# A softmax with fewer vector operations and a new set of starting places in a planned decoder layer

## The chip, the cores and the metric

The kernel runs on one core of one Trainium2 chip. The metric is the device time of one execution in microseconds, as the median of three runs. All arithmetic is in float32.

## The reference

One decoder layer on x of shape (16, 256, 256), with a context of the same shape. Three parts follow each other, each added to its input and then normalised over the last axis.

```python
x = layernorm(x + attn(x))            # a causal, weighted running mean
x = layernorm(x + xattn(x, ctx, ctx)) # correlation by FFT, the 5 best shifts
x = layernorm(x + ffn(x))             # 8 experts, two branches, a router
```

The change touches two softmax-like places. In the first part, the scores are a column slice of the input projection after a causal convolution of four taps with a bias, times a scale for each of the 32 heads, limited and exponentiated:

```python
z = conv(x @ in_proj_w, conv_w) + conv_b       # 4 taps for each channel
s_raw = z[..., -K:]                            # one score for each of 32 heads
p = exp(clip(score_scale * s_raw, -20.0, 20.0))
# p times a weight over time, and running sums of p*re, p*im and p
```

In the second part, each head has the mean correlation of query and key at every shift; the five largest are kept and their softmax weighs five rolled copies of the values:

```python
w, idx = top_k(corr_mean, 5)
w = softmax(w, axis=-1)
out = sum of w[k] * roll(V, idx[k])
```

## The kernel before

The 16 batch rows are taken as 8 pairs. Each pair goes through seven stages, and each is a function of the pair number:

- `front`: the input projection, the convolutions and the scores. The scores of both rows of a pair lie in one tile `sc` (128 partitions, 256 times). `convolve` does the first tap with its bias on ScalarE and three more taps as three VectorE operations; then come the two scale-and-limit operations, the exponential, the weight over time (`tw`, in the profile `dist`) and the running sum `den`.
- `body`: the running sums of the cosine and sine parts. It holds the heaviest VectorE work: scans, products and one fused step on tiles of 128x1024 (`sn`, `cs`, `ge`). It feeds the matmuls `y` and `ss`, and ends in `out_ps` and a layernorm.
- `context` (place "ctx"): the spectra of the context, matmuls `dft_ps` and `kv_ps`; their results go to HBM for pairs 1 to 7.
- `back`: the loads that bring these spectra back.
- `attention` (place "att"): the spectrum of x, the correlation, `choose` (top five and softmax on tiles of 32 partitions: `corr`, `top`, `m8`, in the profile `m`), and the rolled values.
- `router`: the running sum of x, `h_ps`, and the weights of the experts.
- `experts` (place "expert"): the matmuls `c_ps`, `v_ps` and `u_ps`, the last layernorm, the store.

Weights of the experts are first multiplied together by `fold_weights` (place "fold", matmuls `w_ps`). Setup code ahead of the stages loads the small parameters: `pv` is one tile of 45 columns with convolution taps (`C_CW`), biases (`C_CB`), the scores' scale (`C_SCALE`) and others. Columns 24 to 27 of the taps and column 6 of the biases belong to the scores.

No operation is issued where it is written. The objects `V`, `S`, `G`, `T` and `Y` (VectorE, ScalarE, GpSimd, TensorE, and the SyncE queue of DMAs) note each operation, with a rank. The rank comes from the table `PLACES`: for each stage a length and eight beginnings, one for each pair; the rank of an operation is the beginning plus a share of the length. When everything is noted, `Work.run` plans three times. `forward` walks through time with a cost for each operation and lets each engine take the ready operation with the lowest rank; `backward` goes from the end and works out when each operation is due. The due times are the ranks of the next pass. The plan with the shortest planned span is issued, and each engine then runs its instructions in that order and no other. Table loads of ScalarE are put in where the order needs them.

```python
length, *begin = PLACES[stage]
return begin[pair] + part * length
...
for n in range(passes):
    order, starts, span = self.forward(rank, late)
    if best is None or span < best[0]:
        best = span, order, starts
    rank = late = self.backward(starts, span)
```

Because each operation is issued by `give`, nearly all instructions have the same source line in the profile, L452 (`call(*args, **kw)`); table loads have L450. They are told apart by the names of their tiles. Buffers are few where it matters: two of each of `sn`, `cs` and `ge`, one `y` and one `ss` bank, four banks `fps` shared by the other matmuls.

Of the kernel before, what the change touches and what calls it, by code (L numbers as in the profile page):

```python
# [15 lines left out]
AF = mybir.ActivationFunctionType  # L16
ALU = mybir.AluOpType
# [19 lines left out]


PLACES = {
    "front": (0.95, 1.25, 4.3, 4.1, 4.0, 6.3, 4.8, 6.35, 8.75),  # L40
    "body": (0.35, -1.65, 1.6, 3.25, 1.95, 5.25, 3.85, 7.05, 8.6),
    "ctx": (0.85, 2.48, 1.4, 1.55, 1.9, 4.7, 0.3, 2.05, 2.55),
    "back": (3.4, -8.35, -6.05, -8.95, -7.9, -4.75, -7.45, -5.0, 0.8),
    "att": (0.1, -2.35, -3.95, -2.7, -6.8, 1.0, -0.0, 0.7, 3.5),
    "router": (0.35, 0.35, -2.05, 3.45, 4.3, 6.0, 5.65, 6.85, 5.55),
    "expert": (1.18, 3.85, 3.95, 5.85, 5.8, 8.6, 5.95, 9.15, 13.2),
    "fold": (6.5, 1.66),
}
EARLY, SLABS, XT_BUFS, ZC_BUFS, KBUFS, VBUFS, X_BUFS = 3, 19, 1, 4, 2, 3, 9
AHEAD = range(1, NP)  # L50
# [6 lines left out]
C_CW = 0  # L57
C_CB = 28
C_SLOPE = 35
C_SCALE = 36  # L60
# [53 lines left out]
class Work:  # L114
# [67 lines left out]
    @staticmethod  # L182
    def place(stage, pair, part):
        length, *begin = PLACES[stage]
        return begin[pair] + part * length
# [270 lines left out]
def decoder_kernel(ctx: ExitStack, tc: tile.TileContext, a: dict, out: bass.AP):  # L456
# [5 lines left out]
    V, S, G, T, Y = (  # L462
        Later(work, name, eng)
        for name, eng in (
            ("DVE", nc.vector), ("ACT", nc.scalar), ("POOL", nc.gpsimd), ("PE", nc.tensor), ("SP", nc.sync)
        )
    )
# [16 lines left out]
    def load(name, shape, chunks=False, pool=const, eng=Y, tag=None):  # L484
        t = pool.tile(shape, F32, name=name, tag=tag or name)
        eng.dma_start(out=t, in_=chunked(name) if chunks else a[name])
        return t

    def new(pool, shape, tag, bufs=1, name=None):
        work.apart()  # L490
        return pool.tile(shape, F32, name=name or tag, tag=tag, bufs=bufs)

    def slab(shape, name):
        return new(ff, shape, "slab", SLABS, name)

    def m_bank(name):
        return new(m_ps, [P, 512], "mps", 2, name)

    def f_bank(name):
        return new(f_ps, [P, 512], "fps", 4, name)  # L500

    def split(ps, n=2):
        return ps.rearrange("p (c d) -> p c d", c=n)
# [12 lines left out]
    pv = load("pv", [P, NPV], eng=G)  # L516
# [19 lines left out]
    def cumsums(dst, src):  # L536

        V.tensor_tensor_scan(dst, again[:, : dst.shape[1]], src, 0.0, ALU.mult, ALU.add)
# [17 lines left out]
    S.activation(tw, tw, AF.Exp, scale=sp[:, 0:1])  # L556


    dl = pv[:, C_DL : C_DL + 3]
    dw = const.tile([P, 8], F32, name="dw", tag="dw")  # L560
    V.tensor_reduce(dw[:, 4:5], dl, AX.X, ALU.max)
# [28 lines left out]
    def convolve(zc, ps, ci):  # L590

        cw = pv[:, C_CW + 4 * ci : C_CW + 4 * ci + 4]
        S.activation(zc, ps, AF.Identity, bias=pv[:, C_CB + ci : C_CB + ci + 1], scale=cw[:, 3:4])
        for s in (1, 2, 3):
            V.scalar_tensor_tensor(
                zc[..., s:], ps[..., : L - s], cw[:, 3 - s : 4 - s], zc[..., s:], ALU.mult, ALU.add
            )
# [4 lines left out]
    def front(p):  # L602
        place = lambda f: work.place("front", p, f)
        work.rank = place(0.0)
        xT = [slab([P, 2, L], "xc") for c in range(2)]
        for c in range(2):
            Y.dma_start(out=xT[c], in_=a["xT"][p][:, c])
        work.rank = place(0.2)


        ps = m_bank("sc_ps")
        for c in range(2):
            for par in range(2):
                for j in range(2):
                    q = 32 * (2 * j + par)
                    T.matmul(
                        ps[q : q + 32, :L], w_sc[:, c, par, :], xT[c][:, j, :], start=c == 0, stop=c == 1
                    )
        sc = new(mx, [P, L], "sc")
        convolve(sc, ps[:, :L], 6)  # L620
        V.tensor_scalar(sc, sc, pv[:, C_SCALE : C_SCALE + 1], 20.0, ALU.mult, ALU.min)
        V.tensor_scalar(sc, sc, -20.0, None, ALU.max)
        pw = sc
        S.activation(pw, sc, AF.Exp)
        V.tensor_tensor(pw, pw, tw, ALU.mult)
        den = new(mx, [P, L], "den", 2)
        cumsums(den, pw)
        V.tensor_scalar(den, den, 1e-4, None, ALU.max)

        zcs, gs = [], []  # L630
        for m in range(4):
            work.rank = place(0.4 + 0.15 * m)
            zc = new(mx, [P, 2, L], "zc", ZC_BUFS)
            ps = m_bank("in_ps")
            for c in range(2):
                T.matmul(ps, w_in[:, c, m * P : (m + 1) * P], xT[c], start=c == 0, stop=c == 1)
            convolve(zc, split(ps), m)
            zcs.append(zc)
            if m < 2:
                g = new(mx, [P, 2, L], "g", 3)  # L640
                S.activation(g, zc, AF.Identity, bias=dw[:, 1:2], scale=dw[:, 3:4])
                G.tensor_tensor(g, g, zc, ALU.mult)

                ph = new(mx, [P, 2, L], "ph", PH_BUFS)
                for j in range(2):
                    for u in range(2):
                        Y.dma_start(
                            out=ph[64 * u : 64 * u + 64, j, :],
                            in_=pw.rearrange("(n r) t -> n r t", r=8)[8 * j : 8 * j + 8, 2 * m + u]
                            .unsqueeze(1)  # L650
                            .to_broadcast([8, 8, L]),
                        )
                V.scalar_tensor_tensor(g, g, dw[:, 0:1], ph, ALU.add, ALU.mult)
                gs.append(g)

        for m in (2, 3):
            zc = zcs[m]
            S.activation(zc, zc, AF.Silu)
            gate = zcs[m] = new(mx, [P, 2, L], "gate", 3)
            for j in range(2):  # L660
                for h in range(2):
                    Y.dma_start(out=gate[64 * j : 64 * j + 64, h, :], in_=zc[64 * h : 64 * h + 64, j, :])
        made[p] = zcs, gs, den
# [299 lines left out]
    def choose(prod):  # L963


        NHP = 2 * NH
        ps = f_bank("corr_ps")
        for i in range(3):
            T.matmul(ps[:NHP, :L], prod[:, i, :], c_corr[:, i, :], start=i == 0, stop=i == 2)
        T.matmul(ps[:NHP, L : L + 1], prod[:, 0, :], c_mean, start=True, stop=True)  # L970
        corr = new(at, [NHP, L], "corr")
        top = new(at, [NHP, 8], "top")
        m8 = new(at, [NHP, 8], "m8")
        rest = new(at, [NHP, L], "rest")
        S.copy(corr, ps[:NHP, :L])
        S.copy(top[:, 0:1], ps[:NHP, L : L + 1])
        V.max(m8, corr)
        V.tensor_copy(m5[:, :TOPK], m8[:, :TOPK])
        V.match_replace(rest, m5, corr, -FAR)
        V.tensor_scalar(m8, m8, top[:, 0:1], None, ALU.add)  # L980
        V.tensor_scalar(top[:, 1:2], m8[:, 0:1], -1.0, None, ALU.mult)
        V.tensor_tensor(top[:, 2:3], top[:, 1:2], top[:, 0:1], ALU.add)
        S.activation(m8, m8, AF.Exp, bias=top[:, 1:2])
        S.activation(corr, corr, AF.Exp, bias=top[:, 2:3])
        V.tensor_reduce(top[:, 3:4], m8[:, :TOPK], AX.X, ALU.add)
        V.reciprocal(top[:, 4:5], top[:, 3:4])
        V.scalar_tensor_tensor(corr, rest, -FAR, corr, ALU.is_equal, ALU.mult)

        we = new(at, [NHP, 2, P], "we")
        r = top[:, 4:5]  # L990
        S.activation(corr[:, P:], corr[:, P:], AF.Identity, scale=r)
        V.scalar_tensor_tensor(we[:, 0, :], corr[:, :P], r, corr[:, P:], ALU.mult, ALU.add)
        V.scalar_tensor_tensor(we[:, 1, :], corr[:, :P], r, corr[:, P:], ALU.mult, ALU.subtract)
        ps = f_bank("w_t_ps")
        for c in range(2):
            T.transpose(ps[:, c * NHP : (c + 1) * NHP], we[:, c, :], ident[:NHP, :NHP])
        wT = new(at, [P, 2, NHP], "wT")
        S.copy(wT, split(ps[:, : 2 * NHP]))
        ps = f_bank("w_f_ps")
        for i in range(3):  # L1000
            for o in range(2):
                T.matmul(
                    ps[64 * o : 64 * o + 64, i * NHP : (i + 1) * NHP], f_roll[:, o, i, :], wT[:, o, :],
                    start=True, stop=True,
                )
        wf = new(at, [P, 3, NHP], "wf")
        S.copy(wf, split(ps[:, : 3 * NHP], 3))
        return wf, split(ps[:, : 3 * NHP], 3)
# [201 lines left out]
    for p in range(NP):  # L1210
        for stage in (front, body, context, back, attention, router, experts):
            stage(p)
# [138 lines left out]
```

## Time and profile before

| what | value |
|---|---|
| time, median of 3 runs | 856.03 us (855.74 to 857.06) |
| the profiled execution, its own time | 857.1 us |
| its span, first to last instruction | 855.3 us |
| mean granted TensorE clock | 0.989 |
| TensorE busy | 812.4 us, 95% |
| VectorE busy | 700.0 us, 82% |
| ScalarE busy | 581.8 us, 68% |
| GpSimd busy | 256.9 us, 30% |

A row of the profile gives an engine, an operation, the tile it writes and the tiles it reads, the count, the busy time, the mean of one in nanoseconds, and the engine's idle time just ahead of it with what ended that. PE is TensorE, PEld its weight loads, DVE is VectorE, ACT ScalarE, POOL GpSimd, and SP the SyncE queue. PEclk is the granted TensorE clock, where 1 is full speed. Matmuls overlap each other, so a busy PE can hold small gaps that are not seen as idle.

### The profile page before, as it was taken

Reading aid. Unit: us, or ns where it says so; the run is one execution under the profiler, and the core shown is the slowest. Engines: PE = TensorE matmul, PEld = TensorE weight load, DVE = VectorE, ACT = ScalarE, POOL = GpSimd, SP = SyncE. Lnnn points to the kernel's source line nnn. Section 1 sums busy time; section 2 is a strip of 40 time slices with the busy share of each in tenths; the row PEclk is TensorE's granted clock in tenths of the full one; section 3 lists DMA queues with packets and bytes.
Section 4 is the critical chain, followed back from the end, with each engine's and each line's share of the span. In section 5 each row is a group of like instructions: output and inputs, shape, how many; then the busy total and the mean of one; then the engine's idle time right before and its main releaser. Section 6 shows DMA issues by size and latency. Waiting matters only on the chain.

```text
span 855.3 us, 12062 instructions
## 1 busy us (share of the span) xinstructions
PE 812.4 (95%) x4180; PEld 459.1 (54%) x4180; DVE 700.0 (82%) x1200; ACT 581.8 (68%) x862; POOL 256.9 (30%) x301
## 2 busy tenths in 40 slices
PE   4899989989999999999999999999999999999994
PEld 1355554455345564566445745565457457548453
DVE  5799599989998989998999999998979784472431
ACT  3899749777996798675987698678967632712601
POOL 7541356546122051243301501634004111221000
PEclk9899999999999999999999999999999999999997
DMA  8974675574376346633654456426463601130040
GB/s 270 328 177 107 192 196 170 145 200 124 75 173 144 74 102 145 161 85 59 168 124 110 92 116 150 124 50 163 107 138 66 150 22 47 53 72 1 25 99 25
DMA packets 58572, 103.30 MB, mean 121 GB/s; under 512 B 7744, under 2 KB 24160, under 8 KB 58512
## 3 DMA queue, kind: packets, MB, share of 16 engines
q1 hardware_dynamic: 48912, 71.85, 36.3%
q0 software_dynamic: 9600, 30.69, 11.3%
q8 instruction: 33, 0.54, 0.3%
q14 instruction: 27, 0.22, 0.1%
HBM read 28.06 MB, written 11.53 MB: 46 GB/s over the span
## 4 chain that ended last, share of the span: by engine, by line
PE 65%; DVE 13%; ACT 8%; DMA 7%; issue 4%; POOL 1%; SPq 1%; POOLq 0%; DVEq 0%; ACTq 0%
PE u_ps L452 13%; PE v_ps L452 10%; PE c_ps L452 9%; PE h_ps L452 6%; PE kv_ps L452 4%; DVE cs L452 3%; PE in_ps L452 3%; PE ss L452 3%; PE y L452 3%; ACT cs L452 2%; DVE sn L452 2%; PE q_ps L452 2%; PE out_ps L452 2%; DMA sn<-zc 2%; PE dft_ps L452 2%
## 5 line engine op out<-in xcount | busy, mean ns | idle before, releaser
L452 PE MATMUL c_ps<-fcT,w_c 128*128 128x512 f32 x256 | 120.2, 602 | 1.7 <-DVE dx L452 0.8
L452 PE MATMUL v_ps<-fxT,w_v 128*128 128x512 f32 x256 | 119.3, 600 | 1.7 <-ACT e L452 1.4
L452 PE MATMUL u_ps<-u_o,e 128*128 128x256 f32 x512 | 116.6, 382 | 0.3 <-DVE pp L452 0.3
L450 ACT ACT_TABLE_LOAD x89 | 114.2, 1283 | 1.6
L452 PEld LDWEIGHTS u_ps<-u_o,e 128*128 128x128 f32 x512 | 95.6, 190 | 19.9 <-issue 7.4
L452 DVE TENSOR_TENSOR_SCAN cs<-again,cs 128x1024 f32<-128x1024 bf16 x32 | 77.8, 2432 | 0.0
L452 PEld LDWEIGHTS c_ps<-fcT,w_c 128*128 128x128 f32 x256 | 46.5, 190 | 55.6 <-issue 46.6
L452 DVE SCALAR_TENSOR_TENSOR zc<-in_ps,pv,zc 128x510 f32<-128x510 f32 (+2 forms) x96 | 70.1, 736 | 6.3 <-ACT zc L452 5.6
L452 PEld LDWEIGHTS v_ps<-fxT,w_v 128*128 128x128 f32 x256 | 46.7, 190 | 53.0 <-issue 43.9
L452 DVE TENSOR_TENSOR_SCAN sn<-again,sn 128x1024 f32<-128x1024 bf16 x32 | 74.2, 2320 | 0.2
L452 PE MATMUL in_ps<-xc,in_proj_w 128*128 128x512 f32 x128 | 65.0, 636 | 5.1 <-DVE zc L452 4.9
L452 PE MATMUL kv_ps<-Wkv,specc 128*128 128x512 f32 x128 | 60.6, 608 | 0.9 <-DVE ks L452 0.4
L452 POOL TENSOR_TENSOR pp<-qf,kf 128x512 f32<-128x512 f32 (+1 forms) x32 | 45.1, 1429 | 52.4 <-ACT qf L452 37.3
L452 PE MATMUL h_ps<-fxT,w_h 128*128 128x512 f32 x128 | 59.4, 604 | 0.0
L452 DVE TENSOR_TENSOR e<-e,v_ps 128x512 f32<-128x512 f32 x64 | 43.0, 674 | 17.5 <-PE v_ps L452 17.3
L452 POOL TENSOR_TENSOR t<-vf,wf 128x256 f32<-128x256 f32 x32 | 22.6, 726 | 107.9 <-ACT wf L452 80.9
L452 POOL DMA_DIRECT2D out<-x x16 | 11.7, 731 | 131.9 <-ACT x L452 131.7
L452 POOL TENSOR_TENSOR g<-g,zc 128x512 f32<-128x512 f32 x16 | 24.0, 1497 | 83.0 <-ACT g L452 82.0
L452 ACT ACTIVATE sn<-sn,theta_col 128x512 f32<-128x512 f32 x64 | 44.7, 718 | 5.3 <-DMA sn<-zc 5.3
L452 DVE SCALAR_TENSOR_TENSOR cs<-cs,sn 128x1024 f32<-128x1024 f32 x32 | 40.3, 1259 | 9.2 <-ACT cs L452 9.2
L452 DVE TENSOR_TENSOR sn<-sn,ge 128x1024 f32<-128x1024 f32 x32 | 42.9, 1342 | 5.6 <-DMA ge<-g 3.8
L452 DVE TENSOR_TENSOR cs<-cs,ge 128x1024 f32<-128x1024 f32 x32 | 45.3, 1417 | 0.0
(220 smaller groups left out, 1589.4 us busy)
## 6 DMA issues: line engine op xcount, KB each, us to landing
sn<-zc SPq DMA_DIRECT2D x64, 256.0 KB
ge<-g SPq DMA_DIRECT2D x64, 256.0 KB
wb<-fwT SPq DMA_DIRECT2D x64, 256.0 KB
xc<-in_xT SPq DMA_DIRECT2D x16, 256.0 KB
ct<-in_ctx SPq DMA_DIRECT2D x16, 256.0 KB
x<-in_x POOLq DMA_DIRECT2D x16, 256.0 KB, 4.2
ph<-sc SPq DMA_DIRECT2D x64, 64.0 KB
gate<-zc SPq DMA_DIRECT2D x64, 64.0 KB
```

Of the source, the lines that this page charges most:

```text
L450: self.scalar.preload_act_table_set(self.TABLES[table])
L452: call(*args, **kw)
```

## The change

The scale of the scores is multiplied once, in the setup, into their taps and their bias in `pv`. In `front`, the operation that multiplied by the scale and applied the upper limit goes away, and both limits become one operation. In `choose`, the eight largest values are no longer shifted by the mean correlation; the negated, shifted maximum is worked out in one operation from the unshifted maximum, and the exponential of the eight takes its bias from column 2 instead of column 1 of `top`. All numbers of `PLACES` are replaced as well, save a few that happen to agree, so each of the three planning passes starts from other ranks.

```diff
 PLACES = {
-    "front": (0.95, 1.25, 4.3, 4.1, 4.0, 6.3, 4.8, 6.35, 8.75),
-    "body": (0.35, -1.65, 1.6, 3.25, 1.95, 5.25, 3.85, 7.05, 8.6),
-    "ctx": (0.85, 2.48, 1.4, 1.55, 1.9, 4.7, 0.3, 2.05, 2.55),
-    "back": (3.4, -8.35, -6.05, -8.95, -7.9, -4.75, -7.45, -5.0, 0.8),
-    "att": (0.1, -2.35, -3.95, -2.7, -6.8, 1.0, -0.0, 0.7, 3.5),
-    "router": (0.35, 0.35, -2.05, 3.45, 4.3, 6.0, 5.65, 6.85, 5.55),
-    "expert": (1.18, 3.85, 3.95, 5.85, 5.8, 8.6, 5.95, 9.15, 13.2),
-    "fold": (6.5, 1.66),
+    "front": (1.0, 2.05, 4.35, 3.85, 4.2, 5.55, 6.45, 6.3, 7.95),
+    "body": (0.5, -0.5, 1.55, 3.3, 1.5, 4.5, 4.65, 7.05, 7.6),
+    "ctx": (1.0, 2.03, 0.6, 1.2, 1.55, 3.2, 2.35, 1.7, 2.05),
+    "back": (1.35, -6.65, -5.65, -8.75, -9.0, -4.35, -5.75, -2.55, -0.65),
+    "att": (1.75, -3.0, -3.85, -3.8, -5.45, -2.0, -1.05, -0.75, 1.35),
+    "router": (0, 2.0, -2.7, 3.75, 2.9, 3.85, 6.6, 7.65, 4.35),
+    "expert": (1.23, 3.65, 3.65, 5.65, 6.25, 7.5, 7.5, 10.2, 12.05),
+    "fold": (2.0, 2.26),
 }
...
     S.activation(tw, tw, AF.Exp, scale=sp[:, 0:1])
 
 
+    for lo, n in ((C_CW + 24, 4), (C_CB + 6, 1)):
+        V.tensor_scalar(pv[:, lo : lo + n], pv[:, lo : lo + n], pv[:, C_SCALE : C_SCALE + 1], None, ALU.mult)
...
         convolve(sc, ps[:, :L], 6)
-        V.tensor_scalar(sc, sc, pv[:, C_SCALE : C_SCALE + 1], 20.0, ALU.mult, ALU.min)
-        V.tensor_scalar(sc, sc, -20.0, None, ALU.max)
+        V.tensor_scalar(sc, sc, 20.0, -20.0, ALU.min, ALU.max)
         pw = sc
         S.activation(pw, sc, AF.Exp)
...
         V.match_replace(rest, m5, corr, -FAR)
-        V.tensor_scalar(m8, m8, top[:, 0:1], None, ALU.add)
-        V.tensor_scalar(top[:, 1:2], m8[:, 0:1], -1.0, None, ALU.mult)
+
+        V.tensor_scalar(top[:, 1:2], m8[:, 0:1], top[:, 0:1], -1.0, ALU.add, ALU.mult)
         V.tensor_tensor(top[:, 2:3], top[:, 1:2], top[:, 0:1], ALU.add)
-        S.activation(m8, m8, AF.Exp, bias=top[:, 1:2])
+        S.activation(m8, m8, AF.Exp, bias=top[:, 2:3])
         S.activation(corr, corr, AF.Exp, bias=top[:, 2:3])
```

## The prediction

> **What bounds the kernel now.** I read the page's busy shares and its chain first, then a table of busy time for five stretches, then the waits of TensorE inside two of them, and last the groups of the edited operations.
>
> The page's first part and its chain:
>
> ```profile
> PE 812.4 (95%) x4180; PEld 459.1 (54%) x4180; DVE 700.0 (82%) x1200; ACT 581.8 (68%) x862; POOL 256.9 (30%) x301
> ...
> PE 65%; DVE 13%; ACT 8%; DMA 7%; issue 4%; POOL 1%; SPq 1%; POOLq 0%; DVEq 0%; ACTq 0%
> ```
>
> TensorE bounds the kernel. It is idle for only 855.3 - 812.4 = 42.9 us, and the chain spends 65% on it and 13% on VectorE. The busy time of each engine by stretch says where the 42.9 us lie:
>
> ```profile
> 0.00:42.80 42.80, 27.37 (x95) 11.43 (x96) 28.01 (x65) 24.22 (x34) 28.36 (x49) 0.92 0.94 299
> 42.80:256.60 213.80, 202.45 (x1120) 109.06 (x1119) 194.95 (x272) 177.53 (x281) 90.34 (x105) 0.99 0.60 156
> 256.60:640.00 383.40, 378.80 (x2032) 216.43 (x2031) 357.00 (x617) 295.59 (x413) 105.39 (x105) 1.00 0.50 118
> 640.00:833.80 193.80, 193.57 (x892) 114.25 (x891) 116.80 (x238) 82.06 (x131) 31.32 (x40) 1.00 0.25 59
> 833.80:855.30 21.50, 10.25 (x49) 7.92 (x47) 3.29 (x12) 2.37 (x5) 1.45 (x2) 0.80 0.07 24
> ```
>
> The columns are the stretch, its length, then the busy time of PE, PEld, DVE, ACT and POOL, the granted clock, the DMA share and GB/s. TensorE's idle time is 15.4 us in the start-up, 11.35 in the second stretch (5.3% of it), 4.6 in the third (1.2%), 0.2 in the fourth, and 11.2 in the tail. VectorE is 91% and 93% busy in the second and third stretches and 60% in the fourth. So up to about 640 us two engines are nearly full together, and the order of the work decides how often TensorE runs dry; after that only TensorE counts. Who is waited for:
>
> ```profile
> PE sc_ps L452 <- DMA w_sc<-in_w_sc: 8.1, 1, 8.1
> PE in_ps L452 <- DVE zc L452: 4.9, 3, 3.6
> PE y L452 <- DVE cs L452: 3.3, 4, 2.5
> PE out_ps L452 <- DVE gate L452: 1.8, 1, 1.8
> PE w_f_ps L452 <- ACT wT L452: 0.9, 1, 0.9
> PE y L452 <- DVE top L452: 0.7, 1, 0.7
> ```
>
> The reader is to see that the waits are short and scattered: 8.1 us is the arrival of the first weights, which stays, and 3.6 us of `in_ps` is the start-up's wait for the convolution on VectorE. The two lines nearest to `choose` come to 1.6 us in all.
>
> **The change part by part.** First the operations, whose rows are there:
>
> ```profile
> L452 DVE TENSOR_SCALAR sc<-sc 128x256 f32<-128x256 f32 x8 | 3.2, 400 | 0.0
> L452 DVE TENSOR_SCALAR sc<-sc,pv 128x256 f32<-128x256 f32 x8 | 2.7, 342 | 0.0
> L452 DVE TENSOR_SCALAR m<-m,top 32x8 f32<-32x8 f32 x8 | 2.1, 264 | 0.9
> L452 DVE TENSOR_SCALAR top<-m 32x1 f32<-32x1 f32 x8 | 1.0, 131 | 0.0
> L452 DVE TENSOR_SCALAR sp<-sp 128x1 f32<-128x1 f32 x10 | 2.0, 202 | 0.0
> ```
>
> Scores: of the two passes over 128x256 one stays. The new one has two constants and no scalar from memory, like the pass `sc<-sc` in the first row (400 ns by mean, 282 by median, since one of the eight took 1236). No row has two constant limits; I bound it between 282 and the 342 of the pass with a scalar operand and take the form of the existing limit. What goes is then the pass with the scale, 8 x 0.342 = 2.7 us.
>
> A page's price for that pass is lower: the Trainium skill, "VectorE: DVE Perf Modes", section on the errata of SBUF-source operations, gives 58 cycles plus elements over the mode's factor at 0.96 GHz, which for 256 elements at its factor of 2 is (58 + 128) / 0.96 = 194 ns, an estimate. That would make the saving 8 x 0.194 = 1.6 us. The trace has 342 ns for this very pass, so I use 2.7.
>
> `choose`: the shift of the eight goes (2.1 us), and the 131 ns negation becomes an addition with a scalar operand and a negation. The nearest row with a scalar operand on one column is `sp<-sp` at 202 ns; bounds are 131 and the 264 of `m<-m,top`. I take 202: 8 x 0.07 = 0.6 us comes back. The exponential of the eight now waits for column 2, one 140 ns VectorE operation later than column 1, but one operation of 219 ns (median) ahead of both has gone, so neither exponential starts later.
>
> Setup: two operations on `pv`, four columns and one, about 0.21 us each by the `sp` row; 0.4 us. They need only `pv`, which lands at 6.99 us; VectorE has an idle stretch of 1.8 us until `theta_col` lands at 9.28, and the first reader, ScalarE's first tap, starts at 10.11 when `sc_ps` is done. That idle stretch hides them. If the plan puts them behind the VectorE operation that waits for `w_ri` (10.65), the first tap and all of the score's chain wait some 0.6 us; behind them in VectorE's queue would stand the logarithm series `sp` and the convolutions.
>
> VectorE's sum: 2.7 + 2.1 - 0.6 - 0.4 = 3.8 us of 700, 0.5%. What reaches the end is less. In the start-up VectorE runs without a break from 10.7 to 19 us and TensorE waits for it, so one saved pass counts in full, 0.34 us at most. Of the other 3.5 us I count the chain's share of VectorE, 13%: 0.45 us. Together 0.8 us. The bounds are 0, if all of it lies beside other work, and 3.8 if none does. No instruction on TensorE, GpSimd or the SP queue is added or removed, and no wait is added elsewhere.
>
> Second, the order. New starting ranks move potentially every instruction on every queue, the 1200 VectorE operations and the loads and stores on SP and GpSimd too. No row prices that; I bound it by the idle time. A gain can at most remove the idle time of the middle, 11.35 + 4.6 + 0.2 = 16.2 us, and a few of the start-up's microseconds (15.4 less 8.1 for the first weights). The matmul work is the same, and the tail is the last pair's layernorm and store. A loss has no such cap: any microsecond by which VectorE, a buffer or a transfer is late at a matmul is one more, and a thinly used stretch also costs clock. The granted clock is 0.92 between 128.28 and 149.70 us in the trace, behind a stretch (106.90 to 128.30) where PE idled 2.7 of 21.4 us: (1 - 0.92) x 21.4 = 1.7 us.
>
> The Trainium skill, "TensorE: Matmul & The Clock Gate", section on HAM oscillation, has the matching rule: idle gaps over about 3.4 us send the clock to half. By the rule alone no gap of the middle would cost clock, for the longest wait listed there is 2.5 us; the trace shows a dip all the same, behind several short ones. So I price a bad patch as idle plus 1.7 us, not as idle alone, and this speaks against the change.
>
> Which way the order goes I judge from the ranks beside the trace. The heavy VectorE work is `body`, by its rows about (77.8 + 74.2 + 45.3 + 42.9 + 40.3) / 8 = 35 us for each pair. Sorted, the beginnings of `body` were -1.65, 1.6, 1.95, 3.25, 3.85, 5.25, 7.05, 8.6 and become -0.5, 1.5, 1.55, 3.3, 4.5, 4.65, 7.05, 7.6: three couples closer together, the last pair a whole unit earlier. That asks for VectorE work in bunches in the part where VectorE is over 90% full, and `sn`, `cs` and `ge` have two buffers each and `y` and `ss` one bank. The later passes soften this, since they rank by due time. I take as the likeliest that losses like those of the second stretch run on over another 128 us of the third: 128 x (5.3% - 1.2%) = 5.2 us. With the 0.8 us of the operations the change is +4.4 us: 857.1 + 4.4 = 861.5 on the profiled execution. That one stands 1.1 us above the median of the runs, so against the median it is 856.0 + 4.4, about 860.
>
> **The rivals.** (1) The new order serves better, and the lighter VectorE helps: the half of the middle's idle time that lies in scattered waits goes, 8.1 us, plus 0.8: 847. For it speaks that 11.35 us are lost in one stretch, which a better mix could recover as the next stretch shows; against it, that those next 577 us are already at 0.8% idle and can't improve. A milder form ends near 852. (2) The order comes out as good as the old one and only the operations count: 856.0 - 0.8 = 855.2. Against it: so many ranks change that an equal sum would be chance. (3) A large loss: a transfer or bank is held by a queue in a bad place. The place is the third stretch: if TensorE idles there at the second's 5.3% throughout, 383 x 4.1% = 15.7 us, with two clock dips 3.4, and the start-up 2 us longer because loads go out in another order on GpSimd's queue: 21 us, 876 after the saving. It decides from the point where VectorE's lateness exceeds what the four `fps` banks can buffer. (4) The change does not do what it says: if TensorE work sets everything, VectorE's 3.8 us show as idle time there and nowhere else, which ends with case 2.
>
> **How the numbers follow.** A measurement of this kernel tells from no change about 0.2%, 1.7 us. The mild loss has 0.44 and the large one 0.12, slower together 0.56; the equal order has 0.12, within 0.2%; the better order has 0.32. The time is that of the likeliest, 860. The range is to hold eight in ten over cases of both signs: 847, the half of the middle's idle time recovered, to 876, the large loss. The likeliest case alone would range from 858 to 868.
>
> **What would show it.** Right: VectorE busy near 696 us and eight fewer `sc` and `m` operations, eight each; 2 new `pv` operations before 10 us; PE busy still near 812; PE idle between 42.8 and 640 us above 16 us, with waits on `cs`, `gate` or `e` of VectorE grown. Wrong: that idle time below 12 us, or a start-up in which the first `w_ps` or `y` matmul is several microseconds earlier, which would make the kernel faster; or PE busy itself changed by over 3 us, which would say that the order works through how matmuls are packed and not through waits.

## The result: slower by 0.7%, and the profile after

| | before | after |
|---|---|---|
| time, median of 6 runs | 856.54 us | 863.31 us |
| ratio, with its 95% interval | | 1.0073 (1.0051 to 1.0095) |
| the profiled execution, its span | 855.3 us | 861.7 us |
| TensorE busy, idle | 812.4, 42.9 us | 811.8, 49.9 us |
| VectorE busy | 700.0 us | 693.8 us |
| mean granted clock | 0.989 | 0.980 |

The page's busy shares and chain of the changed kernel:

```profile
PE 811.8 (94%) x4180; PEld 463.5 (54%) x4180; DVE 693.8 (81%) x1186; ACT 583.7 (68%) x865; POOL 251.7 (29%) x301
...
PE 38%; DVE 25%; ACT 17%; issue 9%; DMA 6%; POOL 2%; SPq 2%; POOLq 0%; DVEq 0%; ACTq 0%
```

TensorE's busy sum is nearly the same (0.6 us less) and its idle time is 7.0 us longer, so in this sum the 6.4 us of span are idle time of TensorE. The chain points the same way: TensorE's share fell from 65% to 38%, and VectorE and ScalarE took its place. The busy time by stretch (columns as before: stretch, length, PE, PEld, DVE, ACT, POOL, clock, DMA share, GB/s):

```profile
0.00:42.80 42.80, 25.58 (x97) 10.76 (x97) 25.15 (x66) 21.59 (x31) 29.26 (x50) 0.91 0.93 299
42.80:256.60 213.80, 203.42 (x1114) 110.67 (x1115) 188.56 (x259) 174.73 (x275) 81.34 (x101) 0.97 0.58 152
256.60:640.00 383.40, 374.70 (x2035) 220.82 (x2035) 352.25 (x611) 285.31 (x408) 105.91 (x108) 0.99 0.50 118
640.00:833.80 193.80, 191.54 (x864) 108.31 (x863) 123.53 (x238) 99.69 (x149) 33.72 (x40) 1.00 0.26 63
833.80:861.70 27.90, 16.59 (x76) 12.93 (x74) 4.31 (x14) 2.37 (x5) 1.45 (x2) 0.86 0.06 19
```

Subtract the PE column from the length and set it against the kernel before: the start-up idles 17.2 us instead of 15.4, the second stretch 10.4 instead of 11.35, the third 8.7 instead of 4.6, the fourth 2.3 instead of 0.2, and the tail 11.3 instead of 11.2. The differences, +1.8, -1.0, +4.1, +2.0 and +0.1, come to 7 us. These are two single profiles: another one of the changed kernel (run h_after_again below) has 49.4 us of idle time and 810.0 us busy, so a difference of a microsecond or two says little. TensorE's waits name who came late:

```profile
PE sc_ps L452 <- DMA w_sc<-in_w_sc: 7.4, 1, 7.4
PE w_ps L452 <- ACT vf L452: 6.0, 1, 6.0
PE wt_ps L452 <- POOL lg L452: 3.7, 1, 3.7
PE kv_ps L452 <- ACT specc L452: 3.5, 2, 2.9
PE in_ps L452 <- DVE sc L452: 3.5, 1, 3.5
PE w_t_ps L452 <- DVE we L452: 3.3, 4, 1.3
...
PE in_ps L452 <- DVE zc L452: 1.0, 2, 0.6
```

Of the four long waits after the first weights, three are on copies made by ScalarE (`vf`, `specc`) and GpSimd (`lg`), not on VectorE's large operations; the fourth, `in_ps` on `sc`, stands in the start-up, as the wait of 3.6 us for `zc` did before. The wait of `y` on `cs`, 3.3 us before, is down to 0.4.

The granted clock changed too, and neither sum shows it. Ahead of the tail, the kernel before has three stretches at half clock, 10.2 us together (same columns):

```profile
20.51:23.92 3.41, 3.41 (x5) 1.18 (x4) 2.26 (x6) 1.48 (x2) 2.62 (x4) 0.50 0.97 304
34.17:37.57 3.40, 3.12 (x8) 0.85 (x10) 2.89 (x3) 3.37 (x5) 0.86 (x2) 0.50 1.05 353
129.74:133.15 3.41, 3.41 (x20) 1.18 (x20) 3.41 (x6) 3.38 (x6) 3.41 (x5) 0.50 0.29 49
```

The changed kernel has four, 27.3 us together:

```profile
14.26:21.08 6.82, 5.62 (x20) 1.77 (x20) 6.20 (x11) 1.86 (x3) 6.46 (x11) 0.50 0.83 277
41.56:48.38 6.82, 5.71 (x9) 3.15 (x10) 5.40 (x4) 4.85 (x10) 0.00 (x0) 0.50 0.42 115
147.38:154.20 6.82, 5.53 (x44) 2.27 (x46) 6.74 (x12) 6.06 (x11) 0.00 (x0) 0.50 0.19 27
410.20:417.02 6.82, 6.39 (x35) 3.22 (x36) 3.27 (x7) 5.19 (x7) 2.15 (x4) 0.50 0.51 114
```

In the first of these four, the four `in_ps` matmuls of 128x512 take 1061 ns by median, against 592 in the whole kernel. So TensorE's busy sum is no measure of its work alone: 23.3 us of it lie at half clock after the change, 9.9 us before.

The edited operations, in the groups by shape:

```profile
L452 DVE TENSOR_SCALAR sc<-sc 128x256 f32<-128x256 f32 x8 | 2.6, 328 | 0.1
L452 DVE TENSOR_SCALAR top<-m,top 32x1 f32<-32x1 f32 x8 | 1.6, 194 | 0.0
```

One pass over `sc` is left for each pair, the shift of `m` is gone, and the two new operations on `pv` start at 6.57 us, right after `pv` lands and ahead of VectorE's idle time of 1.61 us that ends at 8.88 us.

### The profile page after: what moved, and what is told of

It is laid out like the page before. It is cut to its first block, busy times and chain, and to the rows that moved or that the text cites. A ratio compares the mean times of both kernels' runs of the same rounds, so it can differ in the third digit from the quotient of the medians.

```text
span 861.7 us, 12027 instructions
## 1 busy us (share of the span) xinstructions
PE 811.8 (94%) x4180; PEld 463.5 (54%) x4180; DVE 693.8 (81%) x1186; ACT 583.7 (68%) x865; POOL 251.7 (29%) x301
## 3 DMA queue, kind: packets, MB, share of 16 engines
q0 software_dynamic: 9600, 30.69, 11.3%
## 4 chain that ended last, share of the span: by engine, by line
PE 38%; DVE 25%; ACT 17%; issue 9%; DMA 6%; POOL 2%; SPq 2%; POOLq 0%; DVEq 0%; ACTq 0%
PE v_ps L452 7%; PE u_ps L452 7%; DVE sn L452 6%; PE c_ps L452 5%; DVE cs L452 5%; PE h_ps L452 4%; ACT L450 4%; ACT cs L452 3%; PE kv_ps L452 2%; ACT sn L452 2%; DVE zc L452 2%; ACT x L452 2%; DVE e L452 2%; SPq L452 2%; DMA sn<-zc 2%
## 5 line engine op out<-in xcount | busy, mean ns | idle before, releaser
L452 PE MATMUL v_ps<-fxT,w_v 128*128 128x512 f32 x256 | 121.5, 607 | 1.6 <-DVE e L452 1.0
L452 DVE TENSOR_TENSOR_SCAN sn<-again,sn 128x1024 f32<-128x1024 bf16 x32 | 77.8, 2431 | 0.1
L452 DVE TENSOR_TENSOR_SCAN cs<-again,cs 128x1024 f32<-128x1024 bf16 x32 | 75.0, 2342 | 0.1
L452 PE MATMUL in_ps<-xc,in_proj_w 128*128 128x512 f32 x128 | 63.0, 621 | 4.5 <-DVE sc L452 3.5
L452 DVE TENSOR_TENSOR e<-e,v_ps 128x512 f32<-128x512 f32 x64 | 42.9, 673 | 22.9 <-PE v_ps L452 22.8
L452 POOL TENSOR_TENSOR pp<-qf,kf 128x256 f32<-128x256 f32 (+1 forms) x32 | 44.3, 1405 | 53.0 <-ACT qf L452 46.4
L452 ACT ACTIVATE ge<-sn 128x1024 f32<-128x1024 f32 x32 | 33.8, 1056 | 17.6 <-DVE sn L452 12.2
```

## The experiments

Three theories were tested. Theory 1: the order makes the loss, and the operations help a little. Theory 2: the new operations lose by themselves, because an exponential waits for a later column. Theory 3: a fresh plan lands on some other order whenever the list of operations or the places change, so that the loss belongs neither to the new places nor to the new operations. All ratios below are to the kernel before on the same chip, with 95% intervals; where two of them are subtracted, both intervals count.

### One half of the change at a time, the order kept

To keep an order fixed, the planner was given one kernel's operations, and at the moment of issue the edited ones were exchanged. In the first of the two kernels, the exponential that reads column 2 is also moved behind the operation that writes it, where it stood ahead.

```diff
-            for call, args, kw in o.parts:
+            for call, args, kw in self.instead.get(o, o.parts):
                 call(*args, **kw)
...
         V.tensor_scalar(sc, sc, pv[:, C_SCALE : C_SCALE + 1], 20.0, ALU.mult, ALU.min)
+        work.instead[work.ops[-1]] = []
         V.tensor_scalar(sc, sc, -20.0, None, ALU.max)
+        work.instead[work.ops[-1]] = [(nc.vector.tensor_scalar, (sc, sc, 20.0, -20.0, ALU.min, ALU.max), {})]
```

The same was done in `choose` and for `pv`, and in the opposite direction for the second kernel.

New operations in the old order:

> The new operations, each at the place that the order of the kernel before gave to the operation it replaces; the order of everything else stays (one ScalarE copy of fwT goes ahead of one exponential). Theory 1, the order makes the loss: 0 to 3.8 us below the kernel before, my sum says 0.8 below, ratio 0.9991. Theory 2, the new operations themselves lose (the exponential of the eight waits for column 2): 3 us or more above the kernel before, ratio over 1.003. VectorE busy falls by about 3.8 us either way.

Measured: 855.93 us, ratio 0.9993 (0.9970 to 1.0016). Theory 2 falls: the operations do not lose. The middle of the result is 0.6 us of gain, where the sum said 0.8, but the interval holds zero as well. The page:

```profile
PE 809.1 (95%) x4180; PEld 458.8 (54%) x4180; DVE 695.4 (81%) x1186; ACT 580.9 (68%) x862; POOL 260.7 (31%) x301
```

VectorE did 700.0 - 695.4 = 4.6 us less in its own profile, of which next to nothing shows at the end.

Old operations in the new order:

> The order of the changed kernel with the old operations put back into the places of the new ones. Theory 1: 0.8 us above the changed kernel, so about 864, ratio to the kernel before 1.008 (1.006 to 1.011). Theory 2: the loss goes with the new operations, so about 857, ratio 1.000.

Measured: 867.27 us, ratio 1.0112 (1.0084 to 1.0141). The loss is all in the order. It is just above the expected range, and larger without the new operations than with them (1.0073); the intervals overlap, so the 0.4% between the two, some 3.3 us that the lighter VectorE would be worth in this order, is likely but not established.

### The places and the operations, each planned afresh

In the first kernel the changed one got the old `PLACES`, in the second the kernel before got the new ones; the planner then did its three passes.

> The new operations with the old places, planned afresh. Theory 1 in the narrow form, that the new places are worse than the old ones: within 2 us of the kernel before, ratio 0.998 to 1.002. Theory 3, that any fresh plan moves the time by several microseconds, whichever places: 4 us or more away from the kernel before, on either side, likely above (860 to 866).

Measured: 905.94 us, ratio 1.0563 (1.0530 to 1.0596). TensorE's waits in it:

```profile
PE y L452 <- DVE cs L452: 7.3, 5, 2.6
PE y L452 <- DVE sn L452: 7.2, 4, 2.9
PE w_ps L452 <- ACT w_c L452: 6.5, 3, 5.4
PE fx_ps L452 <- ACT x L452: 6.4, 2, 6.2
PE wo_ps L452 <- ACT aT L452: 5.4, 6, 2.2
```

A list that is 14 VectorE operations shorter (16 gone, two new), with every place as it was, cost 5.6%, by waits of every kind, a 6.2 us one near the end among them. The size was a miss: no theory had said more than 866.

> The old operations with the new places, planned afresh. Theory 1 in the narrow form: near the changed kernel, 862 to 865, ratio 1.006 to 1.010. Theory 3: again another order with its own stalls, not near the changed kernel, anything from 856 to 875; I guess 866.

Measured: 881.38 us, ratio 1.0285 (1.0252 to 1.0317). Also a miss of size, and against the narrow form of theory 1: with the old operations the new places are far worse than with the new ones. Theory 3 holds for these two sets and two lists: each of the two crossed pairs is worse than both matched ones.

The size need not have been a surprise. `Work.run` keeps the shortest of its three plans, and the planning code in each kernel file gives that planned span (in the planner's own costs, not a measurement). The last row is the kernel of the last experiment.

| kernel | planned | against before | measured | against before on its chip |
|---|---|---|---|---|
| before | 825.8 us | | 856.5 us | |
| changed | 827.8 us | +1.9 us | 863.3 us | +6.8 us |
| new operations, old places | 873.2 us | +47.4 us | 905.9 us | +48.6 us |
| old operations, new places | 854.9 us | +29.0 us | 881.4 us | +24.0 us |
| new operations, third places | 817.2 us | -8.7 us | 847.5 us | -10.0 us |

The plan orders all five kernels as the chip does. It also shows which pass was issued: the second one in the kernel before, but the first one in the changed kernel (827.8 us, then 835.8 and 835.4), whose ranks come straight from `PLACES`.

### Single waits of the changed order

The changed kernel ran again, beside kernels in which one or a few instructions of its order were moved or given to another engine.

> The changed kernel unaltered, run beside the next three so that they can be compared on one chip. Both theories: 1.005 to 1.010 of the kernel before.

Measured: 863.14 us, ratio 1.0071 (1.0044 to 1.0097).

First the wait near 407 us. Its piece of the timeline in the changed kernel (start, duration, engine, operation, and in brackets the idle time before it):

```profile
406.71 2.27 DVE L452 TENSOR_TENSOR_SCAN cs<-again,cs 128x1024 f32<-128x1024 bf16 x1
...
406.91 3.67 POOL L452 COPY lg<-lg 128x512 f32<-128x512 f32 x1 [16.14 <-PE w_t_ps L452]
...
410.63 1.12 PE L452 MATMUL wt_ps<-ident,lg 128*128 128x128 f32 x4 [3.69 <-POOL lg L452]
```

The copy that takes 612 ns by median took 3.67 us beside a VectorE scan and the fused step behind it, and TensorE, whose next matmuls in the issued order needed it, stood behind it. The edit gives this one copy to ScalarE in the same place of the order:

```diff
+        third = sorted(self.marks["lg8"], key=lambda o: starts[o][0])[2]
+        self.instead[third] = [(nc.scalar.copy, (lg8, src), {})]
```

> The changed kernel with the third of the eight lg copies (the one of 3.67 us near 407 us) done by ScalarE instead of GpSimd, in the same place of the order. If that copy was slow because VectorE worked on a scan at the same time, as theory 1 has it: the copy takes 0.6 to 0.8 us, the wait of wt_ps falls from 3.69 to under 1 us, the clock dip behind it goes, and the time falls by 3 to 7 us, to 857 to 860. Rival, that TensorE would only wait for something else right after: within 1.5 us of the changed kernel.

Measured: 859.81 us, ratio 1.0033 (1.0017 to 1.0049).

```profile
405.34 2.27 DVE L452 TENSOR_TENSOR_SCAN cs<-again,cs 128x1024 f32<-128x1024 bf16 x1
...
405.87 0.60 ACT L452 COPY lg<-lg 128x512 f32<-128x512 f32 x1
...
406.53 0.66 PE L452 MATMUL wt_ps<-ident,lg 128*128 128x128 f32 x4 [0.95 <-ACT lg L452]
```

Beside the same scan the copy took 0.60 us on ScalarE, and the wait fell from 3.69 to 0.95 us. The time fell by 3.3 us, half of the loss, as theory 1 had it; the wait is 2.7 us shorter, and how much of the rest the clock gave back was not separated. The expectation's clause on the clock was only half right: between 400 and 415 us the granted clock rose from 0.84 to 0.89, not to 1, and the stretch at half clock shrank from 6.8 to 3.4 us. The stall is at GpSimd beside VectorE, which this run shows; the Trainium skill, "GPSIMD Engine Reference", section Specifications, gives a reason that fits, namely that the two engines share their interfaces to SBUF and contend when VectorE reads two SBUF inputs. The other copies agree. Of the 16 `lg` copies of both kernels, five took over 1 us (1.53 to 3.67), and each of these starts 0.15 to 0.20 us into a VectorE operation on 128x1024 with two SBUF inputs and ends 0.4 to 0.5 us after it, or after the one behind it. Three others start as far (0.14 to 0.15 us) into an operation with one input in PSUM (`u_ps`, `v_ps`, `sc_ps`) and took 0.60 to 0.61 us. One of each, from the kernel before:

```profile
316.67 2.28 DVE L452 TENSOR_TENSOR_SCAN cs<-again,cs 128x1024 f32<-128x1024 bf16 x1
316.82 2.54 POOL L452 COPY lg<-lg 128x512 f32<-128x512 f32 x1 [2.27 <-DVE lg L452]
...
741.72 0.68 DVE L452 TENSOR_TENSOR e<-e,v_ps 128x512 f32<-128x512 f32 x1
741.87 0.61 POOL L452 COPY lg<-lg 128x512 f32<-128x512 f32 x1 [1.68 <-DVE lg L452]
```

Then the start-up's wait of 5.95 us on `vf`. In ScalarE's order six large operations of `body` and a table load stood between the copy to `kf` and this one; it was moved in front of them.

```diff
+        kf, vf = self.marks["kv0"]
+        order.remove(vf)
+        order.insert(order.index(kf) + 1, vf)
```

> The changed kernel with one ScalarE copy (the first pair's last copy of kv_ps to vf) moved ahead of five large ScalarE operations that its order put before it; all else in its place. If the 5.95 us wait of w_ps on that copy is a part of the loss, as theory 1 has it: the wait shrinks below 2 us, and the time falls by 3 to 8 us (the wait, and part of the half-clock stretch behind it), to 856 to 860. Rival, that the start-up is bound by the transfers and VectorE anyway and the wait costs nothing: within 1.5 us of the changed kernel.

Measured: 864.32 us, ratio 1.0089 (1.0057 to 1.0122). The rival was right in its number. TensorE's longest waits in that run:

```profile
PE w_ps L452 <- ACT w_v L452: 7.6, 1, 7.6
PE sc_ps L452 <- DMA w_sc<-in_w_sc: 7.5, 1, 7.5
```

`w_ps` now waited 7.6 us for `w_v`, a copy a little further down the same queue. So the next kernel moved `vf` and both `w_v` copies, as far ahead as their matmuls allow:

> The changed kernel with the copy to vf and also the two copies to w_v right behind it moved ahead in ScalarE's order, as early as their matmuls allow. Theory 1, the start-up's stall is part of the loss and vf alone was not enough because w_v stood behind the same five large operations: the wait of w_ps near 36 us falls below 3 us and the time by 2 to 6 us. Rival, that the matmuls delayed there are not due before VectorE lets body go on: the wait shrinks but TensorE idles later by as much, within 1.5 us of the changed kernel (862 to 865).

Measured: 862.11 us, ratio 1.0055 (1.0032 to 1.0078), 0.16% below the changed kernel's 1.0071, within the intervals. In its profile, of the fastest of its runs (859.2 us), the stall near 36 us is down to 0.8 us, and a wait of 3.3 us on `w_h`, a copy further down, has come behind it: TensorE is busy 28.97 us in the start-up instead of 25.58. The second stretch gives 2.3 of these 3.4 us back, busy 201.12 us instead of 203.42. So neither side is settled: by the ratios the stall is worth about 1.4 us, and with both intervals anything from nothing to some 4 us.

Both moves in one kernel, `vf` and the `lg` copy:

> Both of the moves before, in one kernel. If the two waits are separate losses: the sum of the two gains, 6 to 13 us under the changed kernel, 851 to 857, so at or below the kernel before. Rival: the gains overlap or vanish, above 859.

Measured: 860.25 us, ratio 1.0041 (1.0026 to 1.0056), as the `lg` copy alone. The gains do not add, since one of them was none.

Last the wait of `kv_ps` on `specc` at 143 us. ScalarE's exponentials of `choose`, a table load and one operation of `body` stood ahead of the copy.

```diff
+        exp = min(self.marks["exp"], key=order.index)
+        k = order.index(exp)
+        specc = next(o for o in order[k:] if o in self.marks["specc"])
+        order.remove(specc)
+        order.insert(k, specc)
```

> The changed kernel with one copy to specc (near 145 us) moved ahead of the two exponentials of the first choose and the operation behind them, so that kv_ps need not wait for it. Theory 1: the wait of 2.9 us shrinks below 1 us, and the time falls by 1 to 5 us, more than the wait if the half-clock stretch behind it goes too. Rival: VectorE is the limit there, the time stays within 1.5 us of the changed kernel.

Measured: 863.78 us, ratio 1.0079 (1.0052 to 1.0106). No gain. TensorE's waits and the stretch from 128.28 to 149.70 us:

```profile
PE w_t_ps L452 <- DVE we L452: 6.9, 4, 4.9
```

```profile
128.28:149.70 21.42, 14.28 (x79) 6.89 (x82) 21.42 (x31) 18.68 (x29) 9.58 (x11) 0.93 0.69 180
```

The same stretch of the changed kernel:

```profile
128.28:149.70 21.42, 15.17 (x82) 7.25 (x80) 21.42 (x29) 18.02 (x28) 9.98 (x12) 0.95 0.74 192
```

The wait on `specc` is down to 0.7 us, and TensorE waits 4.9 us for `we` of VectorE instead. VectorE is busy for all of the 21.42 us in both. The rival holds: in that stretch VectorE is the limit, and a freed ScalarE copy buys nothing.

> The specc move together with the lg copy on ScalarE, which by itself took the changed kernel from 863.1 to 859.8. Theory 1: both gains add, 855 to 858, so level with the kernel before. Rival: as the lg copy alone, 859 to 860.5.

Measured: 859.08 us, ratio 1.0036 (1.0021 to 1.0051). As the `lg` copy alone again, so the rival holds here too.

### A third set of places

If places belong to a list of operations, there should be a better set for this one. This kernel is the changed one with other `PLACES`, whose planned span is 10.6 us shorter (817.2 us against 827.8); nothing else differs.

```diff
-    "body": (0.5, -0.5, 1.55, 3.3, 1.5, 4.5, 4.65, 7.05, 7.6),
-    "ctx": (1.0, 2.03, 0.6, 1.2, 1.55, 3.2, 2.35, 1.7, 2.05),
+    "body": (0.6, -5.5, 1.25, 7.25, 2.55, 3.9, 4.95, 5.55, 9.3),
+    "ctx": (6.5, 1.68, -7.45, -2.05, 4.95, 11.75, 7.55, -0.3, 4.75),
...
```

> The new operations with a third set of places, another starting order for the same planner. If the change's loss lies in its places and not in its operations, a set exists that beats both: I expect 842 to 852, 0.983 to 0.995 of the kernel before. Rival, that the operations stand in the way of a good order: 858 or more.

Measured: 847.45 us, ratio 0.9900 (0.9873 to 0.9926), faster than both kernels, so the new operations do not stand in the way of a good order. Page, and stretches two to four:

```profile
PE 809.9 (96%) x4180; PEld 460.0 (54%) x4180; DVE 691.6 (82%) x1186; ACT 580.8 (69%) x864; POOL 262.2 (31%) x301
```

```profile
42.80:256.60 213.80, 204.79 (x1116) 110.71 (x1115) 197.47 (x265) 177.95 (x277) 91.81 (x103) 0.98 0.60 158
256.60:640.00 383.40, 380.81 (x2078) 223.47 (x2077) 356.93 (x614) 290.62 (x414) 111.27 (x111) 1.00 0.49 116
640.00:833.80 193.80, 193.76 (x876) 112.75 (x877) 109.14 (x230) 84.49 (x132) 27.65 (x35) 1.00 0.26 60
```

TensorE's busy sum is about the same, and ahead of the tail the trace has 13.7 us at half clock, half of the changed kernel's 27.3. TensorE idles 9.0, 2.6 and 0.04 us in the three stretches, and 12.65 us in the start-up (42.80 less the 30.15 us that it is busy there). VectorE gets more of its work done before 256.60 us, 197.5 instead of 188.6 us.

## Why the prediction was right, and where its steps were not

The forecast was slower, by 4.4 us; measured were 6.8 us between the medians and 6.4 us in the profile. Point by point:

**What bounds the kernel** held in the main. The loss shows as 7.0 us more idle time, and TensorE's busy sum moved by 0.6 us only; between 42.8 and 640 us TensorE idles 19.1 us, over the 16 that were named as the sign. But the busy sum hides that 13 us more of it lie at half clock.

**The operations** held. Predicted were 342 ns for the pass that goes; the one that stays takes 328 by mean. The addition in `choose` was put at 202 ns and takes 194, the two `pv` operations at 0.21 us each and take 0.21, hidden where they were expected. The 3.8 us of VectorE became 4.6 with the order fixed and 6.2 in the changed kernel (7.5 in another profile of it). Some 0.6 us of the difference are the limit that stays, whose longest of eight took 1.24 us in the old order, before and after the edit, and 0.59 in the new one. The 0.8 us on the path agrees with 0.9993 and is not told apart from nothing.

**The order's size** was 5.2 us in the prediction. The changed kernel stands 0.80% over the same operations in the old order (1.0073 less 0.9993), 6.9 us, and with both intervals 4 to 10 us; so the size was not clearly off. The third stretch, to which the prediction gave the loss, did take most of it, 4.1 of 7 us, but the start-up took 1.8 and the fourth stretch 2.0, to which it gave nothing.

**The order's mechanism** was the step that failed. The prediction read the bunched beginnings of `body` as VectorE work coming late, and expected the waits on `cs`, `gate` or `e` to grow. The waits on `cs` shrank from 3.3 to 0.4 us, those on `gate` from 1.8 us to none in the list, and only those on `e` of VectorE grew, from 0.3 to 1.0. Between 42.8 and 640 us all listed waits that VectorE ended fell from 9.5 to 6.4 us, and those that ScalarE and GpSimd ended rose from 5.7 to 11.6, the wait on `vf` that ends at 42.67 us not counted. The largest share of the loss that was found is one GpSimd copy that ran beside a VectorE scan, 3.3 us of the total. Where `body` did get in the way, it was in ScalarE's queue, ahead of the copy to `vf`. The prediction also took it that the later planning passes soften the starting ranks; the plan that was issued is that of the first pass. The ranks alone did not give the sign, as the same old places, planned with 14 operations fewer, cost 5.6%; the planned span did (+1.9 us, and +47.4 for that kernel). That the sum came out near the truth is luck in its second term.

**The two rules.** The skill's 194 ns for the pass was below the trace's 342, and the trace served. The same section says that the row comes out too low and that the fixed part measured some 150 cycles; this would make (150 + 128) / 0.96 = 290 ns, an estimate, near the 282 and 288 ns that the limits with constants take by median. On the clock, the rule on idle gaps over about 3.4 us, which spoke for no dip, fits three of the four stretches of the changed kernel: those at 14.26, 41.56 and 410.20 us begin towards the end of gaps of 3.45, 5.95 and 3.69 us. In the kernel before it fits one of three, with a gap of 3.64 us ahead of the one at 20.51 us. It does not fit the others: the longest gap shortly ahead of the one at 147.38 us is 2.86 us, of those at 34.17 and 129.74 us in the kernel before 2.17 and 2.46 us, and with the `lg` copy on ScalarE a stretch of 3.4 us at half clock starts at 408.00 us behind gaps of 1.12 and 0.95 us. The prediction's 1.7 us for the clock of a bad patch was half of the stretch of 3.4 us that it had seen; in the changed kernel each stretch has 6.8 us.

What stays open: some 3 us of the loss beyond the `lg` copy. The moves of `vf`, `w_v` and `specc` do not settle it. How much of the 6.8 us is the clock and how much the waits themselves was not separated. Matmuls at half clock take longer, and there were more of them after the change, yet the busy sum stayed the same; why is not known.

## What to carry to other kernels

When instructions are placed by a planner or by hand-set priorities, an edit of operations and a new order are two changes: measure the edit in the old order first, by exchanging operations at the moment of issue, and only then look for a new order for the new list. In this kernel a table of priorities said little about another list than its own, so the new plan, not the cost of operations, was what the edit risked. Compare the planner's own span before and after: here it put five kernels in the order in which they ran, though it missed 5 of the 6.8 us of this change. And a named wait is worth its length only if nothing else is late behind it: of three waits of 3 to 6 us on copies, removing one returned 3.3 us, and the others moved to the next copy in the queue or to VectorE.

## What the hardware showed beside that

A GpSimd copy of 128x512 that takes 0.61 us by median took 3.67 us beside a VectorE scan of 128x1024 and the operation after it, while ScalarE made the same copy beside the same scan in 0.60 us. One of the eight copies of the changed kernel met this fully, and it carried half of the loss; one other took 1.54 us. In the kernel before the longest took 2.54 us. Three copies that started beside a VectorE operation with one input in PSUM took 0.60 to 0.61 us.
